# Softmax denominators of a masked attention layer: block 14 joins a running sum that transfers keep, and three terms of ones-products are left of four

## Chip, cores and metric

The kernel runs on one core of one Trainium2 chip. The metric is the device time of one launch in microseconds, and lower is better. Before the change, three runs took 3279.57, 3279.77 and 3284.65 us; their median is 3279.77 us. Times in the tables below come from one further execution that was profiled.

## The reference, cut to what matters

`x` has the shape (8, 2048, 256): 8 frames of 2048 rows with 256 channels. One layer of masked attention with 8 heads of 32 channels is followed by a feed-forward part and three layer norms:

```python
qkv = einsum('fnc,ck->fnk', x, w_qkv)              # q, k, v: (F, N, 8, 32)
scores = einsum('fnhd,fmhd->fhnm', q, k) / sqrt(32)
scores = where(adj > 0, scores, -1e9)
attn = softmax(scores, axis=-1)                    # exp(scores) / its sum over m
t = einsum('fhnm,fmhd->fnhd', attn, v)
y = layernorm(x + t)
y = layernorm(y + relu(y @ w1 + b1) @ w2 + b2)
out = layernorm(x + y)
```

The change concerns the sum over m in the softmax, the denominator. All of it is computed in 32-bit floats.

## The kernel before

**Tiling.** The work is cut into 64 groups: 8 frames `f`, 4 chunks `qc` of 512 query rows, and 2 halves `g` of four heads each. A group has 16 items, one for each block `mb` of 128 keys. So there are 1024 items, in one list (`items`). An item's tile `p` has 128 partitions (keys) by 4 x 512 floats (four heads, 512 queries), which is 1 MB. The pool `pp` has 11 buffers for such tiles.

**One item.** TensorE makes the scores of four heads (`scores`, L230) into PSUM; VectorE adds the mask and writes `p` (L233, two instructions); ScalarE takes the exponential in place (`exponentials`, L237); TensorE multiplies with V and accumulates over the 16 blocks (`values`, L249). In step `t` of the main loop the program first lets side work go forward (`advance`), then issues the exponential of item t+1, the scores of item t+2, the values of item t, and what `add_up` wants of item t.

**The denominators.** The exponentials have to be summed over the keys. Summing over the 128 partitions is a product with a matrix of ones on TensorE (`denominator`, L310): four matmuls for each 1 MB tile, one for each head. To need few of them, the 16 tiles of a group are first added up in place, tile upon tile:

- `POOLED` = blocks 0, 3, 6, 8, 11, 13, 15: GpSimd adds blocks 3 to 15 into the tile of block 0 (L271).
- `MOVED` = two chains, 1, 4, 7, 10 and 2, 5, 9, 12: a DMA that accumulates adds each block into the chain's first tile (L268). GpSimd issues it. A chain's next transfer writes the same tile, so it has to wait for the one before.
- `ALONE` = block 14, which is added to nothing.

So there are four ones-products a group: block 14, the chain of block 1, the chain of block 2, and the tile of block 0. In the last group of all, blocks 13 and 15 are terms of their own too.

In what follows, D4, D5, D7 and so on are the transfers of those blocks, P3, P6 and so on the adds of GpSimd, and e14 is the end of the exponential of block 14. [...] GpSimd's order for a group is P3 D4 D5 P6 D7 P8 D9 D10 P11 D12 P13 P15, with steps of the layer norms and the feed-forward part of an earlier chunk between them (L282 to L286, L355, L357, L412, L414, and the transfers L334 and L359 that add the input `x`).

**Side work.** Everything but the items is written as Python generators (`denominator`, `project`, `queries`, `turn`, `feed_forward` and others) in a list `fill`, sorted by due time. `advance` resumes them by a credit: each step adds 2200, a block of four 512-wide matmuls takes 2048, and below 1024 of credit nothing is issued that isn't due. So a step mostly holds one portion of side work, sometimes none, sometimes two. `denominator` starts two steps after the group's last item, and its last term (the tile of block 0) isn't issued before step `t + SUM` with `SUM = 4`. A generator that holds a PSUM bank goes first until it is done.

## Time and profile before

| what | value |
|---|---|
| profiled execution, its time | 3279.45 us |
| its span, first to last instruction | 3277.3 us |
| mean granted TensorE clock | 0.983 |
| TensorE busy | 3112.2 us (95%) |
| VectorE busy | 2737.7 us (84%) |
| GpSimd busy | 2591.2 us (79%) |
| ScalarE busy | 2438.8 us (74%) |
| adds of GpSimd (L271) | 382, 4776 ns each |
| accumulating transfers (L268) | 384, issue 955 ns each |
| records of ones-products (L310, bank `x`) | 2016, 262.8 us busy together |

A matmul of the program leaves two records here, so four matmuls of a term are eight records. "Busy" of TensorE joins overlapping records: four matmuls use four column strips side by side, so eight records of some 600 ns each take 1.04 us together. The span and the time of the profiled execution differ by 2.15 us, which lie before the first and after the last instruction.

### The profile page before, as it was taken

To read this page: it belongs to the slowest core of one execution; us is meant where nothing else is said; L and a number is where in the kernel's file an instruction comes from. 1 tells how busy PE (TensorE), PEld (TensorE's weight loads), DVE (VectorE), ACT (ScalarE), POOL (GpSimd) and SP (SyncE) were. 2 spreads that over 40 slices of the span, in tenths; PEclk is the share of its full clock that TensorE was granted. 3 is DMA by queue.
4 is the path that set the end of the run, shared out by engine and by line. 5 is a ranking of instruction groups with operands and counts; after the bars stand their busy time and mean duration, and the time that the engine had idled before them with its cause. 6 is when DMAs were issued, how large, how long until landed. Compare 5 with 4: busy or idle time off the path is not lost. (4 is left out here: it accounts for less than half of the span.)

```text
span 3277.3 us, 68323 instructions
## 1 busy us (share of the span) xinstructions
PE 3112.2 (95%) x28948; PEld 979.2 (30%) x28948; DVE 2737.7 (84%) x3203; ACT 2438.8 (74%) x1937; POOL 2591.2 (79%) x1357
## 2 busy tenths in 40 slices
PE   7899999999999999999999999999999999999994
PEld 4222323233332223322233323323223323332221
DVE  4888988888888888888888888888888888878994
ACT  3677878777777777777777777777778777777773
POOL 0578888888878888788887888787888788878894
PEclk8899999999999999999999999999999999999997
DMA  9688779778879788788777879878779778877773
GB/s 318 145 177 189 162 179 200 176 178 197 175 174 207 171 189 185 157 197 200 180 173 173 184 179 213 173 167 197 175 179 198 175 172 201 175 164 163 164 161 77
DMA packets 153384, 591.57 MB, mean 181 GB/s; under 512 B 15056, under 2 KB 67792, under 8 KB 103920
## 3 DMA queue, kind: packets, MB, share of 16 engines
q0 software_dynamic: 64560, 435.85, 66.4%
q1 hardware_dynamic: 87696, 149.98, 13.1%
q8 instruction: 229, 3.75, 0.4%
q10 hardware_dynamic: 816, 1.31, 0.1%
q14 instruction: 83, 0.68, 0.1%
HBM read 146.67 MB, written 37.75 MB: 56 GB/s over the span
## 5 line engine op out<-in xcount | busy, mean ns | idle before, releaser
L233 DVE TENSOR_TENSOR p<-s,mask 128x1024 f32<-128x1024 f32 x2048 | 2409.4, 1218 | 395.7 <-PE s L230 190.0
L237 ACT ACTIVATE p<-p 128x2048 f32<-128x2048 f32 x1024 | 1956.2, 1910 | 554.8 <-DVE p L233 486.8
L271 POOL TENSOR_TENSOR p<-p 128x2048 f32<-128x2048 f32 x382 | 1824.0, 4776 | 268.5 <-ACT p L237 266.2
L230 PE MATMUL s<-qT,kT 32*128 32x512 f32 x8192 | 1173.5, 642 | 70.2 <-DVE p L233 65.7
L249 PE MATMUL x<-p,v 128*32 128x512 f32 x8192 | 1097.6, 608 | 14.0 <-ACT p L237 14.0
L268 POOL DMA_DIRECT2D p<-p x384 | 360.0, 955 | 289.4 <-DMA p<-p 94.4
L230 PEld LDWEIGHTS s<-qT,kT 32*128 32x128 f32 x8192 | 321.1, 183 | 679.0 <-DVE p L233 632.4
L249 PEld LDWEIGHTS x<-p,v 128*32 128x32 f32 x8192 | 161.5, 108 | 795.2 <-issue 294.2
L310 PE MATMUL x<-p,ones 128*32 128x512 f32 x2016 | 262.8, 598 | 4.3 <-POOL p L271 2.7
L54 PE MATMUL x<-in,wqkv 128*32 128x512 f32 x1888 | 244.0, 594 | 4.0 <-DMA in<-xd 4.0
L289 ACT ACTIVATE y<-y,nb,rs 128x256 f32<-128x256 f32 x372 | 219.1, 590 | 37.1 <-POOL nb L286 37.1
L278 DVE BATCH_NORM_STATS2 st<-y 128x6 f32<-128x256 f32 x372 | 155.0, 417 | 6.2 <-DMA y<-in_x_dram 6.2
L54 PE MATMUL x<-w2s,hT 128*32 128x256 f32 x2048 | 123.9, 383 | 3.2 <-DVE y L436 2.1
L54 PE MATMUL x<-turned,w1s 128*32 128x512 f32 x992 | 122.9, 592 | 0.2
L54 PEld LDWEIGHTS x<-wqkv,in 128*32 128x32 f32 x3584 | 102.3, 110 | 62.8 <-issue 59.8
L54 PE MATMUL x<-wqkv,in 128*32 128x128 f32 x3584 | 117.0, 273 | 0.0
L310 PEld LDWEIGHTS x<-p,ones 128*32 128x32 f32 x2016 | 65.7, 111 | 160.3 <-issue 145.8
L54 PEld LDWEIGHTS x<-in,wqkv 128*32 128x32 f32 x1888 | 61.3, 110 | 145.8 <-issue 112.1
L283 POOL TENSOR_TENSOR rs<-rs,mhalf 128x4 f32<-128x4 f32 x93 | 97.1, 1044 | 7.8
L54 PEld LDWEIGHTS x<-w2s,hT 128*32 128x32 f32 x2048 | 66.4, 111 | 77.0 <-issue 30.0
L414 POOL TENSOR_TENSOR y<-y,be1b2r 128x1024 f32<-128x1024 f32 x32 | 85.5, 2671 | 0.6
L355 POOL TENSOR_TENSOR y<-y,g2r 128x1024 f32<-128x1024 f32 x31 | 82.3, 2656 | 1.8 <-ACT y L289 1.8
(117 smaller groups left out, 1335.7 us busy)
## 6 DMA issues: line engine op xcount, KB each, us to landing
p<-p POOLq DMA_DIRECT2D x384, 1024.0 KB, 10.5
in<-xd SPq DMA_DIRECT2D x87, 512.0 KB, 10.6
mask<-md SPq DMA_DIRECT2D x248, 128.0 KB, 8.3
y<-in_x_dram POOLq DMA_DIRECT2D x62, 512.0 KB, 8.3
p<-in_adj_dram SPq DMA_DIRECT2D x16, 1024.0 KB, 9.5
out_dram<-y SPq DMA_DIRECT2D x31, 512.0 KB, 5.8
in<-in_x_dram SPq DMA_DIRECT2D x29, 512.0 KB, 15.3
xd<-in SPq DMA_DIRECT2D x28, 512.0 KB, 11.1
```

Of the source, the lines that this page charges most:

```text
L54: nc.tensor.matmul(out[r:r + D], lhsT[:, r:r + D], rhs, start=start, stop=stop)
L230: nc.tensor.matmul(ps2[half][:, j, :], KT[f, mb // TPC, g][r:r + D, (mb % TPC) * P:(mb % TPC + 1) * P], QT[f, qc, g][r:r + D, :], start=Tr ...
L233: nc.vector.tensor_tensor(pt[:, 2 * half:2 * half + 2, :], ps, MK[f, qc, mb // 2][:, mb % 2, None, :].to_broadcast([P, 2, CH]), ALU.add)
L237: nc.scalar.activation(PT[item], PT[item], AF.Exp, scale=1.0 / math.sqrt(D))
L249: nc.tensor.matmul(O[grp][r:r + D, :], V[f, mb // TPC, g][:, mb % TPC, r:r + D], PT[item][:, h, :], start=(mb == 0), stop=(mb == LAST))
L268: nc.gpsimd.dma_start(PT[f, qc, g, chain[0]], PT.pop(item), accum_op=ALU.add)
L271: nc.gpsimd.tensor_tensor(first, first, PT.pop(item), ALU.add)
L278: nc.vector.bn_stats(st, t[:, j, :])
L283: nc.gpsimd.tensor_tensor(rs, rs, cst["mhalf"], ALU.pow)
L289: nc.scalar.activation(t[:, j, :], t[:, j, :], AF.Identity, bias=nb[:, j:j + 1], scale=rs[:, j:j + 1])
L310: nc.tensor.matmul(ps[r:r + D, :], cst["ones"], term[:, h, :], start=(n == 0), stop=(n == len(terms) - 1))
L414: nc.gpsimd.tensor_tensor(y, y, rows(cst["be1b2r"]), ALU.add)
```

## The change

Block 14 becomes the last link of the chain of block 1: its tile is added to that chain's tile by a fifth transfer, D14, which GpSimd issues between P13 and P15. The term of its own is dropped. The chains change places in the list, so the terms now go: chain of block 2, chain of block 1 (with 14), tile of block 0. `denominator` starts three steps after the group's last item, no longer two; the earliest step of its last term stays.

```diff
     POOLED = (0, 3, 6, 8, 11, 13, 15)
-    MOVED = ((1, 4, 7, 10), (2, 5, 9, 12))
-    ALONE = 14
+    MOVED = ((2, 5, 9, 12), (1, 4, 7, 10, 14))
...
     def denominator(f, qc, g, ready):
         grp = (f, qc, g)
-        terms = [PT.pop((f, qc, g, ALONE))] + [PT.pop((f, qc, g, chain[0])) for chain in MOVED + (POOLED,)]
+        terms = [PT.pop((f, qc, g, chain[0])) for chain in MOVED + (POOLED,)]
         if (f, qc, g) == items[-1][:3]:
-            terms[3:3] = [PT.pop((f, qc, g, b)) for b in ENDED]
+            terms[2:2] = [PT.pop((f, qc, g, b)) for b in ENDED]
...
         if mb == LAST:
-            start(t + 2, denominator(f, qc, g, t + SUM), t + SUM + 4)
+            start(t + 3, denominator(f, qc, g, t + SUM), t + SUM + 4)
```

## The prediction

> **What bounds the kernel now.** I read the page's busy times first, then TensorE's timeline, because the end is set by 1024 items in a row.

> ```profile
> span 3277.3 us, 68323 instructions
> ...
> PE 3112.2 (95%) x28948; PEld 979.2 (30%) x28948; DVE 2737.7 (84%) x3203; ACT 2438.8 (74%) x1937; POOL 2591.2 (79%) x1357
> ...
> q0 software_dynamic: 64560, 435.85, 66.4%
> ```

> TensorE is the fullest engine. The timeline of group 27 (groups counted from 0, so the fourth of the fourth frame), TensorE alone, shows what a portion of side work costs:

> ```profile
> 1451.91 1.07 PE L249 MATMUL x<-p,v 128*32 128x512 f32 x8 [1.30 <-ACT p L237]
> 1452.79 1.90 PE L54 MATMUL x<-turned,w1s 128*32 128x512 f32 x16
> ...
> 1455.69 1.07 PE L249 MATMUL x<-p,v 128*32 128x512 f32 x8
> ...
> 1463.28 1.07 PE L249 MATMUL x<-p,v 128*32 128x512 f32 x8
> 1464.16 1.04 PE L310 MATMUL x<-p,ones 128*32 128x512 f32 x8
> ...
> 1466.20 1.07 PE L249 MATMUL x<-p,v 128*32 128x512 f32 x8
> ```

> From values to values (L249) it is 3.78 us with two portions between (1451.91 to 1455.69) and 2.92 us with one (1463.28 to 1466.20). Items without side work take 2.54 us (median of 63): there TensorE waits for VectorE, whose two mask adds take 2 x 1.218 = 2.44 us. So a portion is worth 0.39 us where it stood alone and 0.86 us where it was the second, not its 1.04 us of busy time. Over all 1023 intervals, those above the median of their kind add up to 86 us of stalls, mostly at a group's ends.

> The timeline of GpSimd in the same group:

> ```profile
> 1442.57 4.89 POOL L271 TENSOR_TENSOR p<-p 128x2048 f32<-128x2048 f32 x1
> ...
> 1449.38 2.35 POOL L412 TENSOR_TENSOR y<-y,g1r 128x1024 f32<-128x1024 f32 x1
> 1451.67 0.91 POOL L268 DMA_DIRECT2D p<-p  x1
> 1452.34 2.67 POOL L414 TENSOR_TENSOR y<-y,be1b2r 128x1024 f32<-128x1024 f32 x1
> 1454.69 14.02 POOL L271 TENSOR_TENSOR p<-p 128x2048 f32<-128x2048 f32 x3
> ```

> The last row is P13, P15 and the next group's P3, 4.67 us each; P13 ends at 1459.5. The exponential of block 14 had ended at 1446.3. GpSimd is 13 us late when it could issue D14. It is late in most groups, though idle 21% of the time: it catches up early in a group, and falls behind again towards its end.

> Landing time of the accumulating transfers, and who waits for them, from the views of line 268 and of the waits:

> ```profile
> DMA to landing us min/median/max: 6.8/10.5/17.3
> ```

> ```profile
> POOL p L268 <- DMA p<-p: 94.4, 36, 6.1
> ...
> DVE p L233 <- DMA p<-p: 49.0, 35, 3.1
> ...
> PEld x L310 <- POOL p L271: 9.9, 14, 1.8
> ```

> Each row: total us, times, longest. GpSimd waits for a chain's transfer before the next; VectorE waits for a buffer that a transfer still reads; the ones-products hardly wait today.

> [...]

> **Removed.** One term in each of 64 groups, but what it frees depends on what moves up. I count the portions between values in the instruction order of both built programs. Two-portion items fall by 40 (33 at 3.78 and 7 at 3.81), one-portion items rise by 17 (2.93), empty ones by 23 (2.54): 17 x 2.93 + 23 x 2.54 - 33 x 3.78 - 7 x 3.81 = **-43 us**. If TensorE were the limit throughout, it would be 64 x 1.04 = 67.

> **Added on GpSimd and DMA.** 64 issues of 0.96 us = 61 us on GpSimd, off the path by themselves (it idles 686 us). P15, queued behind D14, ends about 1 us later, and with it the last term's operand and the next group's P3. 64 MB more on queue 0: 66.4% / 435.85 x 67 = 10% of the span, so the DMA engines go from 80% to some 90%. [...] Buffers: block 14's old tile went free with the first ones-term, now with D14's landing; the next user is block 6 of the next group, two items after the ones-product that waits for the same landing, so this costs nothing of its own.

> **The new wait.** In the new order the second term stands behind the values of the next group's block 2 (40 groups), block 3 (20) or block 5 (3). The first place is four item intervals after the values of block 14, some 13.5 to 14 us after e14; D14 needs GpSimd's lateness plus a landing. I put the new GpSimd order onto the rows of before for groups 24 to 31. It lies between D12 and D14: L355, P13, L357 in 24, 26, 30 (D14 10.2 us after D12); L412, P13, L414 in 25; L357, P13, L359 in 28; P13 alone in 27 and 31. D12 stays where before has it, since the landing of D9 holds it in most groups; in 27 the four norm steps (1.8 us) move into GpSimd's wait ahead of D10 and make it earlier by as much. The landing isn't shown for this place: at least 6.8, at most some 11.5 (median plus 1 for the fuller queue). I take 8.5 where D12 has landed by then and 9.5 where D12 or L359 is in flight, as D9 behind D7 took 8.3 and 9.0 in groups 25 and 24.

> | group | D14 issued | lands | needed | stall |
> |---|---|---|---|---|
> | 24 | 1309.7 | 1318.2 | 1317.3 | 0.9 |
> | 25 | 1357.8 | 1366.3 | 1369.0 | 0 |
> | 26 | 1409.3 | 1418.8 | 1414.8 | 4.0 |
> | 27 | 1457.6 | 1467.1 | 1464.3 | 2.8 |
> | 28 | 1505.0 | 1514.5 | 1511.1 | 3.4 |
> | 29 | after the stall of 28 | | | 0 |
> | 30 | 1607.9 | 1616.4 | 1610.8 | 5.6 |
> | 31 | 1652.5 | 1662.0 | 1660.3 | 1.7 |

> "Needed" is the start of the values before the term plus 1.07 us. Group 29 gets no stall because 28's gives GpSimd time. The sum is 18.4 for 8 groups; the frames with the other mix of places give 20.5 in the same way. 19.5 / 8 x 63 = 154 us. Off this: the 12.6 us that ones-products wait for L271 (9.9 as weight loads, 2.7 as matmuls), since the longer wait covers them, and a third of the 49 us of VectorE's waits for transfers, as GpSimd comes less late after a stall. **+125 us**.

> Sum: 3279.45 - 43 + 125 = **3361 us**, made on the profiled execution, which is 0.3 us from the median of 3279.77.

> **Rivals.**
> - *Covered (faster).* D14 lands before its term everywhere; only the -43 is left: 3236 us. It decides where the new stalls stay under 43 / 63 = 0.7 us a group. For it: TensorE is 95% busy and hardly waits for transfers; the term starts a step later. Against it: 13 us of lateness in group 27 and no landing under 6.8. With 6.8 everywhere the same table gives 6 a group of eight, +52 - 28 - 43, about 3260.
> - *The queue fills (slower still).* At 90% the landings lengthen for all. At 11.5 us for D14 the table gives some 33 for 8 groups: 264 - 28 - 43 = +193, and 3472; together with partial relief, 3430 to 3472. For it: landings reach 17 us today where three transfers overlap. Against it: after D12 no transfer of a chain is due before block 4.
> - *Half way.* Lateness some 2 us below the table, because earlier stalls give GpSimd time in every group, not only 29: stalls about as large as the gain, 3262 to 3300.

> **Chances.** Forecast (3300 to 3430) 0.60; queue fills 0.14; half way 0.14; covered 0.12. What a measurement of this kernel can tell from no change is about 0.2%, 6.6 us. Half way gives 0.03 faster, 0.04 same, 0.07 slower. So faster 0.15, same 0.04, slower 0.81. The range of 3262 to 3445 leaves out the covered case and the top of the filling queue.

> **What would show it.** A row of ones-product weight loads or matmuls waiting for `DMA p<-p` of 100 us or more shows the new wait; under 30 us, I am wrong. TensorE's busy time falls by 60 to 67 us. Intervals with one portion stay at 2.92 at the median. GpSimd's lateness at D14 is 8 to 14 us in most groups, landings 8 to 10 at the median. If landings of all transfers rise by over 1.5 us, the queue fills.

## The result, and the profile after

The changed kernel takes 3514.13 us (median of four runs, 3507.77 to 3515.12). The kernel before took 3279.67 us beside it. The ratio is 1.0713, with a 95% interval of 1.0689 to 1.0737. The change makes the kernel slower by 7.1%. Slower was forecast, but with 3361 us, and the time lies above its range (3262 to 3445). The forecast cost was 81 us, the real one 234.

The page of the changed kernel (line numbers are one lower than before: ones-products L309, accumulating transfers L267, GpSimd's adds L270):

```profile
span 3513.1 us, 67569 instructions
...
PE 3141.8 (89%) x28436; PEld 969.2 (28%) x28436; DVE 2736.5 (78%) x3203; ACT 2437.9 (69%) x1937; POOL 2643.9 (75%) x1421
...
q0 software_dynamic: 73776, 502.96, 71.4%
...
L309 PE MATMUL x<-p,ones 128*32 128x512 f32 x1512 | 223.2, 666 | 192.2 <-DMA p<-p 191.9
...
p<-p POOLq DMA_DIRECT2D x448, 1024.0 KB, 10.0
```

TensorE issues 512 matmul records fewer, and yet it is busy 30 us longer (3112.2 before). That cannot be work, so it is speed: the mean granted clock fell from 0.983 to 0.950. The fourth line has TensorE idle for 192 us ahead of the ones-products. The last line shows that the transfers did not become slower: 10.0 us to landing at the median, 10.5 before.

The waits of the changed kernel (total us, times, longest):

```profile
PEld x L309 <- DMA p<-p: 225.3, 52, 10.2
PE x L309 <- DMA p<-p: 191.9, 53, 9.3
POOL p L267 <- DMA p<-p: 102.8, 31, 6.4
...
PE x L95 <- DMA in<-in_x_dram: 35.1, 5, 11.0
...
DVE p L233 <- DMA p<-p: 10.1, 9, 2.6
```

The first row is idle time of the weight loads, which overlap matmuls (969.2 and 3141.8 us busy, together more than the span of 3513.1); the second is TensorE's own. It is the new wait that was forecast. The third is GpSimd's wait for a chain's earlier transfer (94.4 before). The fourth row was not forecast: TensorE waits for loads of `x` (`in_x_dram`), which it did nowhere in the loop before. The last row fell from 49.0.

One such wait, in group 28, on TensorE's timeline:

```profile
1612.31 1.07 PE L249 MATMUL x<-p,v 128*32 128x512 f32 x8
1621.27 1.94 PE L309 MATMUL x<-p,ones 128*32 128x512 f32 x8 [7.89 <-DMA p<-p]
1623.13 2.09 PE L230 MATMUL s<-qT,kT 32*128 32x512 f32 x8
1625.15 1.19 PE L249 MATMUL x<-p,v 128*32 128x512 f32 x8
1626.16 1.03 PE L309 MATMUL x<-p,ones 128*32 128x512 f32 x8
```

TensorE stands for 7.89 us at the second term: from 1613.40 to 1621.24 the trace has no matmul and no weight load. The four matmuls of that term then take 1.94 us and the scores 2.09, where the usual times are 1.04 and 1.14. The view by windows shows the granted clock around it (1.00, 0.51, 1.00, behind the count of records in brackets):

```profile
core 0: us, PE busy (x), PEclk, DMA share, GB/s
1606.00:1618.60 12.60, 7.27 (x60) 1.00 0.84 167
1618.60:1625.50 6.90, 4.23 (x20) 0.51 0.43 88
1625.50:1632.00 6.50, 6.50 (x53) 1.00 0.82 170
```

So one late transfer is paid twice: by the wait, and by half speed after it.

GpSimd's timeline ahead of that wait:

```profile
1605.51 5.17 POOL L270 TENSOR_TENSOR p<-p 128x2048 f32<-128x2048 f32 x1
1610.02 1.50 POOL L358 DMA_DIRECT2D y<-in_x_dram  x1
1610.60 1.81 POOL L267 DMA_DIRECT2D p<-p  x1
1611.16 5.80 POOL L270 TENSOR_TENSOR p<-p 128x2048 f32<-128x2048 f32 x1
```

The rows are P13, the transfer that adds `x`, D14 and P15. D14 is issued 11.2 us after e14 and lands 10.6 us later, at 1621.2; the ones-product starts then.

**Where the time went.** For every run I took the loop from the first to the last values (L249) and split it, from the records of the trace, into three parts: TensorE idle; the loss at half speed, which is half of TensorE's busy time inside stretches with a granted clock near 0.5; and the rest, which is its work at full clock. The split is of the one profiled execution. The first stretch (34 to 41 us) begins ahead of the loop and is counted whole in every kernel. So 8.5 to 9.6 us of each loss lie before the loop, and each figure of work is too low by as much; differences between kernels change by about 1 us at most.

From before to after the loop goes from 3111.4 to 3340.0 us, idle time from 90.8 to 289.8, the loss at half speed from 24.4 (8 stretches) to 99.4 (40 stretches), and the work at full clock from 2996 to 2951. The loop grew by 228.6 us: +199 idle, +75 at half speed, -45 work. Of the idle part, +188 lies ahead of ones-products (192.2 after, 4.3 before), +35 ahead of the transposes of `x` (L95), and the rest fell by 24. The experiments are read with the same split.

### The profile page after: what moved, and what is told of

It is laid out like the page before. It is cut to its first block, busy times and chain, and to the rows that moved or that the text cites. A ratio compares the mean times of both kernels' runs of the same rounds, so it can differ in the third digit from the quotient of the medians.

```text
span 3513.1 us, 67569 instructions
## 1 busy us (share of the span) xinstructions
PE 3141.8 (89%) x28436; PEld 969.2 (28%) x28436; DVE 2736.5 (78%) x3203; ACT 2437.9 (69%) x1937; POOL 2643.9 (75%) x1421
## 5 line engine op out<-in xcount | busy, mean ns | idle before, releaser
L233 DVE TENSOR_TENSOR p<-s,mask 128x1024 f32<-128x1024 f32 x2048 | 2409.7, 1218 | 631.3 <-PE s L230 436.3
L237 ACT ACTIVATE p<-p 128x2048 f32<-128x2048 f32 x1024 | 1955.5, 1910 | 550.5 <-DVE p L233 460.6
L270 POOL TENSOR_TENSOR p<-p 128x2048 f32<-128x2048 f32 x382 | 1868.3, 4891 | 303.8 <-ACT p L237 303.4
L230 PE MATMUL s<-qT,kT 32*128 32x512 f32 x8192 | 1205.1, 659 | 52.3 <-DVE p L233 43.3
L249 PE MATMUL x<-p,v 128*32 128x512 f32 x8192 | 1109.8, 614 | 7.5 <-ACT p L237 7.5
L267 POOL DMA_DIRECT2D p<-p x448 | 467.7, 1056 | 447.4 <-ACT p L237 243.4
L309 PE MATMUL x<-p,ones 128*32 128x512 f32 x1512 | 223.2, 666 | 192.2 <-DMA p<-p 191.9
L249 PEld LDWEIGHTS x<-p,v 128*32 128x32 f32 x8192 | 162.6, 109 | 813.2 <-issue 312.2
L54 PE MATMUL x<-in,wqkv 128*32 128x512 f32 x1888 | 246.9, 595 | 6.8 <-DMA in<-xd 6.8
L311 ACT COPY dT<-x 128x512 f32<-128x512 f32 x63 | 36.9, 585 | 264.2 <-PE x L309 264.2
L309 PEld LDWEIGHTS x<-p,ones 128*32 128x32 f32 x1512 | 45.4, 118 | 337.1 <-DMA p<-p 225.3
L54 PE MATMUL x<-w2s,hT 128*32 128x256 f32 x2048 | 123.6, 383 | 1.1 <-ACT oT L253 0.7
L54 PE MATMUL x<-turned,w1s 128*32 128x512 f32 x992 | 124.2, 592 | 0.0
L54 PEld LDWEIGHTS x<-wqkv,in 128*32 128x32 f32 x3584 | 102.6, 110 | 67.0 <-issue 51.8
L54 PE MATMUL x<-wqkv,in 128*32 128x128 f32 x3584 | 118.4, 273 | 0.0
L54 PEld LDWEIGHTS x<-in,wqkv 128*32 128x32 f32 x1888 | 61.6, 110 | 148.9 <-issue 112.5
L356 POOL TENSOR_TENSOR y<-y,be2r 128x1024 f32<-128x1024 f32 x31 | 87.6, 2825 | 0.0
L411 POOL TENSOR_TENSOR y<-y,g1r 128x1024 f32<-128x1024 f32 x32 | 87.1, 2723 | 0.1
```

Source lines behind the costliest of these rows:

```text
L54: nc.tensor.matmul(out[r:r + D], lhsT[:, r:r + D], rhs, start=start, stop=stop)
L230: nc.tensor.matmul(ps2[half][:, j, :], KT[f, mb // TPC, g][r:r + D, (mb % TPC) * P:(mb % TPC + 1) * P], QT[f, qc, g][r:r + D, :], start=Tr ...
L233: nc.vector.tensor_tensor(pt[:, 2 * half:2 * half + 2, :], ps, MK[f, qc, mb // 2][:, mb % 2, None, :].to_broadcast([P, 2, CH]), ALU.add)
L237: nc.scalar.activation(PT[item], PT[item], AF.Exp, scale=1.0 / math.sqrt(D))
L249: nc.tensor.matmul(O[grp][r:r + D, :], V[f, mb // TPC, g][:, mb % TPC, r:r + D], PT[item][:, h, :], start=(mb == 0), stop=(mb == LAST))
L267: nc.gpsimd.dma_start(PT[f, qc, g, chain[0]], PT.pop(item), accum_op=ALU.add)
```

## The experiments

Theory W (wait): the cost is the wait of the second term for D14. Theory L (load): the cost is D14's issue and its traffic, wherever it is waited for. Theory S (start; the expectations call it order theory): the cost is the new order of TensorE's work. Except where the text says it, each kernel is the changed one with the edit shown.

**e1_left_out.** Block 14 is in no sum at all; the denominators lack it. Three terms stay, without the transfer.

```diff
-    MOVED = ((2, 5, 9, 12), (1, 4, 7, 10, 14))
+    MOVED = ((2, 5, 9, 12), (1, 4, 7, 10))
+    LEFT = 14
...
+        if mb == LEFT:
+            PT.pop(item)
```

> Three terms, and no transfer for block 14: the block is left out of the denominators. All else is in the order of the changed kernel. It is the removal alone. Wait theory (the loss is TensorE standing at the second term until D14 lands, and its slower clock after it): the removal's own gain is left, 3280 - 43 = 3237 us, between 3225 and 3250. Order theory (the loss comes from the later start and the order of the side work, for instance the late loads of x): stays above 3400. Load theory (the loss is what D14 puts on GpSimd and the DMA engines): also 3237, so this run doesn't part it from the wait theory.

Measured: 3329.48 us, ratio 1.0161 (1.0144 to 1.0178). A miss for every theory: with one term less and no transfer more, the kernel is slower than before. Its waits say where:

```profile
PE x L312 <- DMA p<-p: 42.1, 21, 6.1
...
PE x L95 <- DMA in<-in_x_dram: 30.4, 5, 6.4
```

L312 is the ones-product here. The removal did save its work (2949 us at full clock), but idle time is 153.5 us and the loss at half speed 55.6. Most of the waits at L312 are of the first term. That term is now the chain of block 2, whose D12 is the last transfer that GpSimd issues in this kernel; before the change it was the third of four.

**e2_aside.** D14 is issued in its place, but adds block 14's tile to itself. No term waits for it, and block 14 is missing from the denominators.

```diff
+        if mb == ASIDE:
+            aside = PT.pop(item)
+            nc.gpsimd.dma_start(aside, aside, accum_op=ALU.add)
```

> As the changed kernel, with D14 issued at the same place and of the same size, but it adds block 14's tile to itself, so no term waits for it and D14 doesn't wait for D10; block 14 is missing in the denominators. Wait theory: 3237 us plus what the fuller queue costs, 3240 to 3280. Load theory: stays near 3514, above 3420. The 35 us that transposes wait for loads of x in the changed kernel should be gone if they come from D14's traffic behind a stall, and stay if the order makes them.

Measured: 3373.81 us, ratio 1.0298 (1.0280 to 1.0315), between the two. From its waits (L313 is the ones-product):

```profile
PE x L95 <- DMA in<-in_x_dram: 45.6, 5, 11.3
PE x L313 <- DMA p<-p: 34.7, 17, 5.0
```

Against e1 it is 44 us slower: this is the load. In the loop's idle time it shows ahead of the scores (78.7 us of waits for VectorE, 49.6 in e1) and of the transposes of `x` (45.6 for 30.4), and not ahead of ones-products. Against the changed kernel it is 140 us faster: this is the wait for D14 (in the loop 100 us less idle and 39 less at half speed). It is a net figure, since other waits are longer in e2: those for `x`, and VectorE's for transfers (66.0 us for 10.1). So W has the larger part, L a smaller one that is not nothing, and 52 us are still neither. The waits for `x` stayed, which the expectation had put down to the order.

**e3_start5.** The denominator starts two steps later.

```diff
-            start(t + 3, denominator(f, qc, g, t + SUM), t + SUM + 4)
+            start(t + 5, denominator(f, qc, g, t + SUM), t + SUM + 4)
```

> As the changed kernel, but the terms start five steps after a group's last item instead of three; the whole computation is done. The term with block 14 then stands some two items later (5.8 us). Wait theory: of the 53 waits of the changed kernel, 197 us, about twelve are longer than 5.8 us and keep some 20 us together; few last long enough to slow the clock. 3237 + 20 to 60 = 3257 to 3300 us, if the sums' tiles, held two items longer, don't make VectorE wait for buffers. Load theory: no gain, about 3514. Order theory: a further loss or no gain.

Measured: 3235.70 us (3228.41 to 3240.76), ratio 0.9881 (0.9865 to 0.9898): 1.2% faster than before, and below the range of every theory. From its page and its waits:

```profile
span 3226.6 us, 67566 instructions
...
PE 3056.6 (95%) x28436; PEld 959.7 (30%) x28436; DVE 2733.8 (85%) x3203; ACT 2444.5 (76%) x1937; POOL 2649.8 (82%) x1421
```

```profile
DVE p L233 <- DMA p<-p: 67.7, 41, 3.9
...
PE x L309 <- DMA p<-p: 13.8, 12, 1.9
```

D14's wait is almost gone (13.8 us for 191.9). The waits for loads of `x` are gone too (35.1 us in the changed kernel), so the gain is not W's alone. Idle time (93.1 us) and loss at half speed (21.1) are as before the change, and the saved work is left over. VectorE's waits for transfers rose to 67.7 us, since tiles come free later.

**e4_start_only.** The kernel before with its four terms, but with the other order of the change: the start a step later, and the chains exchanged.

```diff
-    MOVED = ((1, 4, 7, 10), (2, 5, 9, 12))
+    MOVED = ((2, 5, 9, 12), (1, 4, 7, 10))
...
-            start(t + 2, denominator(f, qc, g, t + SUM), t + SUM + 4)
+            start(t + 3, denominator(f, qc, g, t + SUM), t + SUM + 4)
```

> The kernel before with four terms, started three steps after the last item instead of two, and with the chains in the changed order; no D14. Wait theory: within 0.5% of before, 3265 to 3295 us, since the portions per item are counted the same as before. Order theory: near 3400 or above.

Measured: 3323.80 us, ratio 1.0158 (1.0133 to 1.0182). A miss for both theories: this order alone costs 46 us. TensorE's timeline shows a wait that the kernel before does not have; it comes once in six of the seven frames whose `x` is loaded in the loop:

```profile
1818.27 1.07 PE L249 MATMUL x<-p,v 128*32 128x512 f32 x8
1825.32 1.12 PE L95 MATMUL x<-ident,in 128*128 128x128 f32 x4 [5.99 <-DMA in<-in_x_dram]
1826.36 2.09 PE L230 MATMUL s<-qT,kT 32*128 32x512 f32 x8
...
1829.66 1.03 PE L310 MATMUL x<-p,ones 128*32 128x512 f32 x8
```

One load of `x` in each of these six takes 20.4 to 21.0 us to land, in this kernel and in the kernel before. Before the change its transposes came ten items after it was issued (29.3 to 29.9 us): the denominator had started, held its PSUM bank, and so went first. With the start a step later the transposes come first, five items after the issue (20.5 to 21.1 us), and TensorE waits 5.7 to 6.3 us and then runs at half speed. The split agrees: idle +31 us, of it 35.9 ahead of the transposes, half speed +12, work unchanged (2995).

**e5_warm.** In 34 groups 146 blocks of four matmuls with a zero weight matrix are put ahead of the second term, about as many as fit its wait there, so that TensorE keeps its clock.

```diff
+            for _ in range(WARM.get((f * NCK + qc) * 2 + g, 0) if n == 1 else 0):
+                for h in range(4):
+                    r = D * h
+                    nc.tensor.matmul(ps[r:r + D, :], cst["zeros"], terms[0][:, h, :], start=False, stop=False)
```

> The changed kernel with idle work in its waits: in the 34 groups whose second term waited 1.5 us or more in the changed kernel's trace, blocks of four matmuls with weights of zero (1 us each, as many as the wait has whole us, 146 blocks in all) go ahead of that term. They add nothing to the sums. Clock theory [...]: the waits stay as long, but of the 99 us that half-speed stretches cost in the changed kernel some 50 to 65 go: 3450 to 3465 us. Rival (what follows a wait is slow because the pipeline of scores, mask adds and exponentials has to fill again): 3514 us or a little more.

Measured: 3495.26 us, ratio 1.0657 (1.0639 to 1.0675). A miss in size. The loss at half speed fell from 99 to 44 us, so the matmuls put into the waits did keep the clock up, as the clock theory has it (the half speed comes from TensorE's standing). But only 19 us came back (31 between the two profiled executions, on which the split rests). D14 landed no earlier: 20.3 us after e14 at the median, 19.7 in the changed kernel. So a faster TensorE comes to the term earlier and waits there: the 129 us of added work displaced only 105 us of idle time.

**e6_turn_later.** The transposes of `x` are due nine steps after the load, no longer five.

```diff
         nc.sync.dma_start(xc, x[f, c * CH:(c + 1) * CH, :].rearrange("(j p) c -> p j c", p=P))
-        yield 5
+        yield 9
```

> The changed kernel with nine steps instead of five between the load of a chunk of x and its transposes. In the kernel before the load that takes 20 us is met 10 steps later, in the changed kernel and in the one with the start alone 5 steps later. Order theory for this part of the loss: the 35 us of waits for loads of x go, with some 10 us of slow clock behind them: 3460 to 3480 us. If the loads are late because of stalls elsewhere, it stays at 3514.

Measured: 3487.64 us, ratio 1.0631 (1.0609 to 1.0653): 26 us less than the changed kernel, where 34 to 54 were expected. The waits for `x` are gone (35 us before the edit, none after), as expected; but the ones-products wait 7 us longer (198.9 us for 192.2), and the loss at half speed is 6 us larger.

**e7_block13.** Block 13 joins the running sum, and GpSimd adds block 14. (In the last group of all, `ENDED` becomes 14 and 15 to match.)

```diff
-    POOLED = (0, 3, 6, 8, 11, 13, 15)
-    MOVED = ((2, 5, 9, 12), (1, 4, 7, 10, 14))
+    POOLED = (0, 3, 6, 8, 11, 14, 15)
+    MOVED = ((2, 5, 9, 12), (1, 4, 7, 10, 13))
```

> The changed kernel with blocks 13 and 14 exchanged: the fifth transfer is D13, and GpSimd adds block 14. GpSimd's order is then P11 D12 D13 P14 P15, so the last transfer goes out one item earlier and without an add of 4.9 us ahead of it, some 5 to 8 us earlier in all. The order on TensorE is the same. Wait theory: the second term's waits fall from 190 to 20 to 50 us, the slow clock with them; the late load of x (46 us) and the first term's waits stay: 3300 to 3370 us. Load theory: as many transfers and as much work on GpSimd, so little changes: above 3450.

Measured: 3461.05 us, ratio 1.0559 (1.0537 to 1.0582). W's range is missed by 91 us, and the time stands on L's side of the line (above 3450), though only just.

```profile
PE x L309 <- DMA p<-p: 117.7, 58, 5.8
```

The wait fell from 191.9 to 117.7 us and did not vanish: from 173 to 82 us at the second term, while it rose from 19 to 37 at the first. The 74 us less go W's way. The edit did not do what it was meant to: over the 63 groups with three terms, D13 is issued 7.0 us after e14 at the median and D14 in the changed kernel 9.0, so 2 us earlier and not 5 to 8; and D13 takes longer to land, 11.4 us for 10.6. So e7 hardly parts the two theories.

**e8_before_start5.** Is the gain of e3 the later start by itself? The kernel before with start(t + 5, ...), no other edit.

> The kernel before, four terms and no D14, with the terms started five steps after the last item as in the run at 3236 us. By the count of portions between values it should be 9 us slower than before (36 double ones-portions instead of 13, 82 items without any). If the gain of that run comes from the term that is gone: 3280 to 3300 us. If it comes from the later start, for instance because the loads of x fall better: 3230 to 3250 us.

Measured: 3348.98 us, ratio 1.0206 (1.0189 to 1.0223), outside both ranges. No: with four terms the later start costs 69 us. The scores wait 115 us for VectorE (66 before), VectorE 121 us for transfers that hold tiles (49 before), and the transposes of `x` 29 us. The later start paid only with three terms.

**e9_start4 and e10_start6.** The changed kernel with start(t + 4, ...) and start(t + 6, ...).

> The changed kernel with the terms started four steps after the last item, between the changed kernel (3) and the run at 3236 us (5). The second term stands one item, 2.9 us, later. Wait theory: of 176 us that second and third terms wait in the changed kernel, 75 us in 24 waits outlast 2.9 us; most end before the clock halves. 3237 + 75 + 15 = 3327 us, between 3280 and 3360. If the gain of start 5 comes from where side work falls alone, it jumps: near 3236 or near 3470.

> The changed kernel with the terms started six steps after the last item. Wait theory: nothing is left to wait for beyond the 14 us of start 5, so 3220 to 3250 us; a loss against start 5 would come from the sums' tiles, which hold three of the eleven buffers one item longer, and would show as waits of VectorE for transfers.

Measured: 3309.00 us, ratio 1.0094 (1.0068 to 1.0120), and 3243.91 us, ratio 0.9896 (0.9873 to 0.9920), both in the range of W. Idle time ahead of the ones-products is 192, 90, 14 and 0 us for a start of 3, 4, 5 and 6 steps. The waits for loads of `x` are gone from four steps on. From the waits of e10:

```profile
PE s L230 <- DVE p L233: 106.3, 134, 3.9
DVE p L233 <- DMA p<-p: 84.4, 52, 4.6
```

At six steps nothing is left to hide, and the tiles are held longer: VectorE waits longer for transfers to release them, and the scores for VectorE (76.6 us in e3). Five steps is the best of the four, though e3 and e10 lie close.

**e11_left_out_start5.** e1 with start(t + 5, ...): no D14, block 14 missing from the denominators.

> The kernel of start 5 without D14: block 14 is left out of the denominators. The order on TensorE is that of start 5. It prices D14's traffic and issue where no term waits for it. Wait theory: 3215 to 3240 us, at most 20 below start 5. Load theory: 40 us below start 5, as the run with the transfer aside was 44 us above the one that left block 14 out.

Measured: 3200.53 us, ratio 0.9756 (0.9739 to 0.9772). Against e3 it is 35 us, near L's 40: D14 costs that much where TensorE hardly waits for it, and 44 us at three steps (e2 against e1). In the profiled executions the difference is 27 us; TensorE's idle time makes up 19 of it, 14 ahead of ones-products (none here) and 5 ahead of the scores. VectorE's waits for transfers are 31.3 us here and 67.7 in e3, but little of that reached TensorE.

**e12_start_turn_later.** e4 with the edit of e6.

> The run with the later start alone (four terms, no D14, 3324 us), with nine steps instead of five between the load of a chunk of x and its transposes. The portions change too: 24 more items without any, 33 of two or three. If the six waits of some 7 us for loads of x are all of what the start costs: they go, and 3275 to 3295 us is left. If not, above 3305.

Measured: 3315.15 us, ratio 1.0109 (1.0092 to 1.0126). The second branch: the waits at the transposes of `x` fell from 35.9 to 1.4 us, but only 9 us came back. The scores wait 85 us for VectorE (62 in e4) and the values 20 us (11). So e4's wait for `x` is seen in its trace, but taking it away there did not bring its length back. What else that order costs stays open.

All runs in the split of the loop. The times are medians, the rest is of the profiled execution, which lies up to 11 us from the median (e5; 7 in e3):

| kernel | time us | idle | lost at half speed | stretches | work at full clock |
|---|---|---|---|---|---|
| before | 3279.67 | 90.8 | 24.4 | 8 | 2996 |
| e4, four terms, the new order | 3323.80 | 122.0 | 36.4 | 13 | 2995 |
| e12, e4 with later transposes | 3315.15 | 115.5 | 30.3 | 12 | 2998 |
| e8, four terms, start 5 | 3348.98 | 152.7 | 37.4 | 15 | 2996 |
| e1, block 14 left out | 3329.48 | 153.5 | 55.6 | 21 | 2949 |
| e2, D14 not waited for | 3373.81 | 190.0 | 60.2 | 26 | 2949 |
| after, start 3 | 3514.13 | 289.8 | 99.4 | 40 | 2951 |
| e5, matmuls in the wait | 3495.26 | 184.5 | 43.6 | 16 | 3080 |
| e6, later transposes | 3487.64 | 256.2 | 105.1 | 42 | 2952 |
| e7, block 13 in place of 14 | 3461.05 | 244.2 | 75.8 | 34 | 2959 |
| e9, start 4 | 3309.00 | 139.7 | 45.0 | 19 | 2948 |
| e3, start 5 | 3235.70 | 93.1 | 21.1 | 7 | 2943 |
| e10, start 6 | 3243.91 | 107.9 | 29.8 | 11 | 2940 |
| e11, left out, start 5 | 3200.53 | 74.3 | 20.4 | 6 | 2939 |

With three terms the work is 37 to 57 us less than before in every kernel (e5's added matmuls aside). All else that separates these kernels is idle time and half speed.

## Why the prediction was wrong in size

The direction, and the wait that causes most of it, were forecast. Three steps failed. A stall was priced at its length, and the half speed after it at nothing: 75 us. The wait was too small: +125 us were forecast with its deductions, and 164 measured (188 ahead of ones-products, less 24 elsewhere). The later start was priced at nothing: 35 us of new waits for `x` stand in the changed kernel.

**The removed term: right.** -43 us was forecast from intervals, -45 is the change of the work at full clock, which is near it though not the same measure. The medians stayed: 2.92 us for an interval with one portion and 3.78 with two. Empty intervals rose from 63 to 86, the 23 that were counted. It was not 64 x 1.04 = 67, as the prediction said. Its sign for this, TensorE's busy time down by 60 to 67 us, was wrong all the same. It left out the clock: busy time rose by 30. In e3, which loses little at half speed, it fell by 56 (3112.2 to 3056.6): records overlap their neighbours, so that a term adds about 0.87 us (56 / 64).

**The new wait: right in place and mechanism, too small.** That a ones-product that waits holds up all of TensorE was the author's assumption; in group 28 it is so, with nothing of TensorE's in the 7.89 us. For groups 24 to 31 the table gave stalls of 0.9, 0, 4.0, 2.8, 3.4, 0, 5.6 and 1.7, together 18.4 us. Measured are 3.4, 0, 1.8, 4.7, 7.9, 0, 2.0 and 0.9, together 20.7. The lateness of D14 was 6.5 to 13.1 us and its landings 7.4 to 13.5, against 8 to 14 and 8 to 10 forecast. So the sum for this frame was right to 2.3 us, but that is luck: the errors of the single groups, up to 4.5 us, come to 15.5 and cancel. The step to the other frames was too small: "19.5 / 8 x 63" gives 154, and the second terms of all groups wait for 173; groups 56 to 62 alone have 29.7. The term that was mis-sized is the landing: 10.6 us over the 63 groups, at the median and at the mean, above the forecast 8 to 10 and the 8.5 and 9.5 of the table. GpSimd's lateness, 8.6 us at the mean where the table has 9.7, takes part of that back. D12 is still in flight when D14 goes out in 57 of the 63 groups. The lines of before show it in groups 24 and 30 too, where D12 lands at 1310.4 and 1609.4; the table took 8.5 there as if it had landed. Another 19 us are waits of the first term. Of the deductions, the 12.6 us were counted too high: 9.9 of them are idle time of the weight loads, and TensorE's matmuls stood only 4.3 us ahead of ones-products before. The other, 16 us, was too low (VectorE's waits fell by 39, TensorE's idle time elsewhere by 24). In the rival with landings of 6.8, "6 a group of eight" gives 47 by the same step, where +52 stands.

**A term that was missing: the clock.** The prediction reckoned a stall at its length. The stretches at half speed rose from 8 to 40, and their loss by 75 us. Around the end of the 7.89 us wait of group 28 the granted clock was 0.51 for 6.9 us. The trace before has 8 such stretches already, with a loss of 24.4 us, and nothing was priced from them.

**A step costed at nothing: the order.** "The term starts a step later" stood in the prediction as a point for the covered case. In e4, together with the exchange of the chains, it costs 46 us. Its trace shows most of that ahead of the transposes of `x`, which now meet a slow load (+35 us of idle time in the changed kernel too). But taking that wait away returned 9 us there (e12) and 26 in the changed kernel (e6), so the rest stays open. The prediction counted portions from the instruction order of the changed program, but asked only the ones-products what they would wait for.

**The order of the terms: not reckoned.** With the chains exchanged, the first term needs D12 one item earlier than the third term did. e1 shows it: without D14 at all, its ones-products wait 42 us for transfers. In the changed kernel it is 19 us.

**GpSimd's issues and the traffic: "off the path by themselves" was wrong.** They cost 44 us at three steps and 35 at five. The named bound, landings 1.5 us longer for all, was not the way: their median went from 10.5 to 10.0 us. At three steps the cost shows ahead of the scores and of the loads of `x`, at five more ahead of the ones-products (14 us) than of the scores (5).

Two sums lead to the result, and they cut it differently. By the prediction's terms: forecast +82, wait too small by 39, `x` 35, clock 75, together +231, where the loop grew by 228.6. By the experiments: removed work -43 (the forecast; no run shows it alone), the order +46 (e4), the rest of e1 +48, the load +44 (e2 - e1), the wait for D14 with its half speed +140, together +235, where the medians differ by 234. The +48 is what is left between e1 and the first two; that it is the wait for D12 and its half speed is read from e1's trace and was not tried alone. Nor do these steps add in any order: leaving block 14 out makes the kernel 6 us slower at three steps (e1 against e4), and 148 faster at five (e11 against e8, which differ in the order of the chains too).

**The rivals.** The queue did not fill. The covered case was priced at 3236 us, and e3, with a start two steps later than the change has, takes 3235.70. That they meet is in part luck: the price had D14 cost nothing, but e11 without it is 78 us below the kernel before, and D14 takes 35 of them back. Two steps are two intervals of 2.92 us, 5.8 us, which covers 28 of the 41 waits of the second term.

## What to carry to other kernels

A consumer of a transfer has to be put behind the lateness of the engine that issues it plus a landing, here some 20 us after the data are ready (15 to 23 over the groups); two steps of a loop made the difference between 7.1% slower and 1.2% faster. Count a stall of the busiest engine at its length and at what the clock takes afterwards, here 75 us at half speed beside 199 us of idle time. When one step of a credit-driven order moves, look at every other step that changes places with it, and first at those that wait for slow loads.

## What the runs showed of the hardware that was not expected

**A small load can be the slowest.** Of the four loads of `x` in each of six frames, 0.5 MB each, two took 18.9 to 21.4 us to land in the kernel before, and one 5.6 to 6.2; its accumulating transfers of 1 MB took at most 17.3. While one of 21.0 us was in flight in the changed kernel (1477.3 to 1498.3), so were, for a part of that time, D7, D9, D10, D12, a transfer of GpSimd that adds `x`, and three transfers of SP. Beside one of the 5.6 us loads before (at 2290.8) were D12, one that adds `x`, and three of SP. What makes the difference was not tried.
